# Second pass: where ScalarE clips the next unit's k

## The chip, the cores and the metric

The kernel runs on one core of a Trainium2 chip, in one launch, all in float32. The time is the device time of that core in microseconds, as the median of several runs.

## What is computed

Two layers run one after the other on x of shape (8, 256, 64, 64), batch by channels by rows by columns. The first is attention with keys and values from a strided 4x4 convolution. The second, the one that the change is in, is a linear attention with ReLU on q and k:

```
qkv = einsum('oc,bchw->bohw', w_qkv, x)
dw  = conv(qkv, w_dw, 5x5, per channel)
agg = einsum('goi,bgihw->bgohw', w_pw, dw)        # 96 groups of 8 channels
ms  = concatenate([qkv, agg], axis=1)
q, k, v = relu(ms[:d]), relu(ms[d:2d]), ms[2d:]   # per head, d = 8, v padded with a 1
kv  = einsum('bhnd,bhne->bhde', k, v)
out = einsum('bhnd,bhde->bhne', q, kv)
out = out[..., :-1] / (out[..., -1:] + 1e-15)
```

A projection, a normalization by fixed constants and the residual follow. Half of the heads read qkv itself ("raw" in the kernel), the other half read agg, what the 5x5 convolution and the 8x8 mix make of it. The ReLU on k is "the clipping" in what follows.

## The kernel before

Three passes share one program. The first (L575) does layer 0 and the qkv projection and stores qkv in DRAM in several layouts. The second (L961) makes the sums over tokens, kv, for all heads, and the whole output of the agg half. The third (L1279) applies the raw half, projects, and writes the output.

The second pass goes over 64 units: t in 2, k in 4, batch b in 8, one unit being 32 heads' channels of one batch. Its loop (L1225) is a software pipeline. In its step u it works on four units at once: u (convolution of k), p = u - 1 (token sums of agg), q = u - 2 (convolution of q) and r = u - 3 (application of the sums). What the steps of this text touch:

- load_tokens(u) (L1002) loads the raw k of a unit into kq (512 KB) and raw v into vq. kq has two buffers, used in turn.
- positive(u) (L1066) clips kq in place on ScalarE (L1068, 128x1024), then has GpSimd add it up over tokens: reduced (L1059), lines L1061 to L1063, into red_raw, which has one buffer.
- summed_raw(u) (L1104) is 32 small matmuls of kq with vq (L1110). ended_raw(u) (L1153) adds one matmul with red_raw (L1157) and copies the result out on VectorE (L1159, L1160).
- convolve(u, what, i) (L1073) is 16 matmuls into a PSUM bank: what = 1 is k (L1085), what = 0 is q (L1089). There are three banks of the tag cv, taken in turn. Part i = 2 comes first and ScalarE copies it to `both` (L1092). Parts 0 and 1 are added to `both` on VectorE (L1100, s) and clipped on ScalarE (L1101, r).
- summed(u) (L1120) is 32 matmuls of r with vq (L1127), four side by side in the four column strips of the array. A reduction on GpSimd (red_agg, again L1061 to L1063) and small work on VectorE (L1137 to L1145) follow. ended (L1167) and spread (L1175) turn the sums into the block matrix bd, by two small matmuls (L1170, L1177), a copy on ScalarE (rep, L1179) and two products on GpSimd.
- applied(u, par) (L1196) multiplies q by bd into ng (L1201). Then ScalarE's den (L1203), VectorE's reciprocal (L1204), product tok (L1206) and transpose att (L1213) follow each other.
- paired(u, what) (L1020) makes the differences c on VectorE (L1025, L1026), and on GpSimd a copy (L1029).

The source gives the calls in an order, but the framework's planner orders each engine's instructions when the program is built, by its own reckoning of when they can start. An engine then runs its instructions in that order. An instruction given to `tc.keep_in_program_order` stays at its place in the source among its engine's instructions; before, only some stores are given to it. In the order as built before, ScalarE's clipping that stands between r of convolve(q, 0, .) and `both` of convolve(u, 1, 2) is that of k two units ahead of the raw matmuls around it, though the source calls positive(u) at the head of step u.

Of the kernel before, what the change touches and what calls it, by code (L numbers as in the profile page):

```python
# [28 lines left out]
AF = mybir.ActivationFunctionType  # L29
# [931 lines left out]
def second_pass(ctx: ExitStack, tc: tile.TileContext, a, planes, kd, vd, wtd, kvd, attd):  # L961
    nc = tc.nc
# [16 lines left out]
    def bank(tag, name, bufs=1, n=512):  # L979
        return psums[tag].tile([P, n], F32, tag=tag, name=name, bufs=bufs)  # L980

    units = [(t, k, b) for t in range(2) for k in range(4) for b in range(B)]
    n_all = len(units)
# [10 lines left out]
    def load_cells(u, what):  # L994
        t, k, b = units[u]
        home = (second if u % 2 else first) if what else third
        d = home.tile([P, 4, (NB + 1) ** 2], F32, tag=f"d{what}_{u % 2}", name=f"d{what}_{u}")
        nc.sync.dma_start(d, planes[b, 2 * what + t][4 * k : 4 * k + 4].rearrange("g p e -> p g e"))
        grids[u, what] = d.rearrange("p g (y x) -> p g y x", x=NB + 1)


    def load_tokens(u):  # L1002
        t, k, b = units[u]
        kq = (second if u % 2 else first).tile([P, 2, 4, P], F32, tag=f"kq_{u % 2}", name=f"kq_{u}")
        nc.sync.dma_start(
            kq.rearrange("p a c e -> p a (c e)"),
            kd[b][4 * t + k].rearrange("a y (m i) b e -> (y m) a (i b e)", i=2),
        )
        kqs[u] = kq
        vq = (second if u % 3 else first).tile([P, 4, 6 * P], F32, tag=f"vq_{u % 3}", name=f"vq_{u}")  # L1010
        v = vd[b][4 * t + k]
        row = (NB2 + 2) * P
        for r in range(4):
            src = [[2 * row, NB], [4 * P, NB // 2], [1, 6 * P]]
            nc.sync.dma_start(vq[:, r], bass.AP(tensor=v.tensor, offset=v.offset + r * row, ap=src))
        vqs[u] = vq.rearrange("p r (c f h e) -> p r c f h e", c=6, f=4, h=4)
# [3 lines left out]
    def paired(u, what):  # L1020
        d = grids[u, what]
        c = (pairs if what else late).tile([P, 2 + what, 4, (NB + 1) * NB // 2], F32, tag=f"c{what}", name=f"c{what}_{u}")
        v = c.rearrange("p n g (y x) -> p n g y x", x=NB // 2)
        d0, d1, d2 = (d[:, :, :, i : i + NB - 1 : 2] for i in range(3))
        nc.vector.tensor_sub(v[:, 0], d0, d1)  # L1025
        nc.vector.tensor_sub(v[:, 1], d2, d1)  # L1026
        if what:

            nc.gpsimd.tensor_copy(v[:, 2], d1)  # L1029
        cells[u, what] = c  # L1030
# [28 lines left out]
    def reduced(u, what, t):  # L1059
        r = mid.tile([P, 4, P], F32, tag=f"red_{what}", name=f"red_{what}_{u}", bufs=1)  # L1060
        nc.gpsimd.tensor_tensor(r, t[0], t[1], ALU.add)  # L1061
        nc.gpsimd.tensor_tensor(r[:, :2], r[:, :2], r[:, 2:], ALU.add)
        nc.gpsimd.tensor_tensor(r[:, 0], r[:, 0], r[:, 1], ALU.add)  # L1063
        reds[u, what] = r[:, 0]

    def positive(u):  # L1066
        kq = kqs[u]
        nc.scalar.activation(kq, kq, AF.Relu)  # L1068
        reduced(u, "raw", (kq[:, 0], kq[:, 1]))


# [1 line left out]
    def convolve(u, what, i):  # L1073
        t, k, b = units[u]
        c, w, d = cells[u, what], wt[t, k, what], grids[u, what]
        ps = bank("cv", f"cv{what}_{u}_{i}", 3)
        for g in range(4):
            for da in range(2):
                n = 2 * da + i if i < 2 else 4 + da
                cols = slice(da * (NB // 2), da * (NB // 2) + P)  # L1080
                x = d[:, g, da : da + NB, 1:NB:2] if i == 2 and not what else c[:, i, g, cols]
                m = w[:, g, n * P : (n + 1) * P]
                out = ps[:, g * P : (g + 1) * P]
                if what:
                    nc.tensor.matmul(out, x, m, start=(da == 0), stop=(da == 1))  # L1085
                else:
                    if i == 2:
                        out = out.rearrange("p (y x) -> p y x", y=NB)
                    nc.tensor.matmul(out, m, x, start=(da == 0), stop=(da == 1))  # L1089
        if i == 2:  # L1090
            both = between.tile([P, QB], F32, tag="both", name=f"both{what}_{u}")
            nc.scalar.copy(both, ps)  # L1092

            r = (sides if what else two).tile([P, 2, 4, P], F32, tag=f"r{what}", name=f"r{what}_{u}")
            state[u, what] = (r, both)
            (kts if what else qs)[u] = r
        else:
            r, both = state[u, what]
            s = sides.tile([P, QB], F32, tag="s", name=f"s{what}_{u}_{i}")
            nc.vector.tensor_add(s, ps, both)  # L1100
            nc.scalar.activation(r[:, i].rearrange("p h n -> p (h n)"), s, AF.Relu)  # L1101


    def summed_raw(u):  # L1104
        kq, vq = kqs.pop(u), vqs[u]
        ps = bank("raw", f"raw_{u}")
        for i in range(8):
            r, c = i // 4, i % 4
            for f in range(4):
                nc.tensor.matmul(  # L1110
                    ps[f * D0 : (f + 1) * D0, :D0],
                    kq[:, r, c, f * D0 : (f + 1) * D0],
                    vq[:, r + 1, c + 1, f].rearrange("p h e -> p (h e)"),
                    start=(i == 0),
                    stop=(i == 7),
                )
        raws[u] = ps
# [45 lines left out]
    def stored_raw(u):  # L1163
        t, k, b = units[u]
        tc.keep_in_program_order(nc.sync.dma_start(kvd[b, t][:, k], mraws.pop(u)))
# [30 lines left out]
    def applied(u, par):  # L1196
        t, k, b = units[u]
        q, bd = qs[u], bds[u]
        pn = bank("ng", f"ng_{u}_{par}", 1, 1024).rearrange("p (h n) -> p h n", h=4)
        for h in range(4):  # L1200
            nc.tensor.matmul(pn[:, h, : P + 16], q[:, par, h], bd[:, h], start=True, stop=True)  # L1201
        den = late.tile([P, 2, 4, 16], F32, tag="den", name=f"den_{u}_{par}")
        nc.scalar.activation(den[:, 0], pn[:, :, P : P + 16], AF.Identity, bias=eps)  # L1203
        nc.vector.reciprocal(den[:, 1], den[:, 0])  # L1204
        tok = late.tile([P, 16, D0], F32, tag="tok", name=f"tok_{u}_{par}")
        nc.vector.tensor_tensor(  # L1206
            tok.rearrange("p f (h e) -> p h f e", e=D1),
            pn[:, :, :P].rearrange("p h (f e) -> p h f e", e=D1),
            den[:, 1].unsqueeze(3).to_broadcast([P, 4, 16, D1]),
            ALU.mult,  # L1210
        )
        att = two.tile([P, 512], F32, tag="att", name=f"att_{u}_{par}", bufs=4)
        nc.vector.transpose(att, tok.rearrange("p f e -> p (f e)"))  # L1213
        done[u, par] = att


    def stored(u, par):
        t, k, b = units[u]
        c0 = P * t + D0 * k
        tc.keep_in_program_order(  # L1220
            nc.sync.dma_start(attd[b][c0 : c0 + D0, par].rearrange("c j n -> j c n"), done.pop((u, par)))
        )

    paired(0, 1)
    for u in range(n_all + 3):  # L1225
        p, q, r = u - 1, u - 2, u - 3
        now, was, conv, out = u < n_all, 0 <= p < n_all, 0 <= q < n_all, 0 <= r < n_all
        if now:
            positive(u)
            if u > 0:  # L1230
                summed_raw(u)
        if u + 1 < n_all:
            load_tokens(u + 1)
        if 0 < p < n_all:
            load_cells(p, 0)
        if was:
            stored_raw(p)
        if r > 0:
            stored(r - 1, 0)
            stored(r - 1, 1)  # L1240
        if was:
            summed(p)
        if now:
            convolve(u, 1, 2)
        if out:
            applied(r, 0)
        if u + 1 < n_all:
            paired(u + 1, 1)
        if now:
            convolve(u, 1, 0)  # L1250
            if u == 0:
                summed_raw(u)
            ended_raw(u)
            convolve(u, 1, 1)
        if u + 2 < n_all:
            load_cells(u + 2, 1)
        if was:
            ended(p)
        if conv:
            paired(q, 0)  # L1260
            convolve(q, 0, 2)
        if out:
            applied(r, 1)
        if conv:
            convolve(q, 0, 0)
        if was:
            spread(p)
        if conv:
            convolve(q, 0, 1)
        if now and u + B < n_all:  # L1270
            b = units[u][2]
            load_weights(u + B - b, 1 if b < 4 else 0, b % 4)
# [354 lines left out]
```

## Time and profile before

| what | us |
|---|---|
| median of 3 runs | 4081.7 (4080.74 to 4086.17) |
| span of the profiled run | 4083.3 |
| TensorE matmul busy | 3951.4 |
| VectorE busy | 1901.1 |
| ScalarE busy | 1651.8 |
| GpSimd busy | 1193.4 |
| the second pass, first raw matmul to last row of ng | 2139.2 to 3427 |
| one clipping, L1068 (64 of them) | 1.06 |

In the profile, PE is TensorE's matmuls and PEld its weight loads, DVE is VectorE, ACT ScalarE, POOL GpSimd, SPq the queue that issues the DMAs. A row of the trace in order of time has start, duration, engine, line of the kernel, operation, output<-input, shape and count; merged rows carry the count x. A bracket at its end gives how long that engine was idle before it and what ended the wait. A wait in a list is told as the waiting row, the arrow, and the row that released it. Float32 matmuls stand in the trace as two records each.

### The profile page before, as it was taken

The page shows a single profiled execution, that of the slowest core. Times are in us where ns is not written, and L with a number is a line of the kernel's source. Part 1 is how long each engine was busy: PE and PEld are TensorE (multiplying, and loading weights), DVE is VectorE, ACT ScalarE, POOL GpSimd, SP SyncE. Part 2 cuts the span into 40 slices and gives each one's busy share as a digit, 9 for nine tenths or more (in the row PEclk, how much of TensorE's full clock was granted, in tenths as well). Part 3 has the DMA queues.
Part 4 walks back from the last instruction along what each step waited for, and adds up shares of the span by engine and source line. Part 5 has one row for each costly group of instructions (what it writes and reads, how often), then busy time and mean ns, then how long its engine had stood idle before and what let it go on. Part 6 is the DMA issues. An engine that isn't in the chain of part 4 may idle for free. (4 is left out here: it accounts for less than half of the span.)

```text
span 4083.3 us, 69412 instructions
## 1 busy us (share of the span) xinstructions
PE 3951.4 (97%) x27266; PEld 2340.8 (57%) x27266; DVE 1901.1 (47%) x2724; ACT 1651.8 (40%) x3505; POOL 1193.4 (29%) x1234
## 2 busy tenths in 40 slices
PE   8999999999999999999998899999999998999998
PEld 4433434434334343343347788888888886555655
DVE  2554344343443434344445555555555554444443
ACT  2345454453554545545542222222222223445544
POOL 2323233233333323323334343333433431000000
PEclk9999999999999999999999999999999999999999
DMA  7655435344353443534449877777777766777674
GB/s 234 205 178 163 117 91 151 94 121 133 94 147 100 114 137 100 139 97 116 136 117 267 233 207 215 215 204 227 214 206 226 200 178 166 225 210 229 196 235 136
DMA packets 588320, 691.31 MB, mean 169 GB/s; under 512 B 62160, under 2 KB 431312, under 8 KB 583760
## 3 DMA queue, kind: packets, MB, share of 16 engines
q1 hardware_dynamic: 587984, 686.79, 59.2%
q8 instruction: 216, 3.54, 0.4%
q14 instruction: 120, 0.98, 0.1%
HBM read 412.54 MB, written 274.10 MB: 168 GB/s over the span
## 5 line engine op out<-in xcount | busy, mean ns | idle before, releaser
L786 POOL TENSOR_TENSOR e<-e,e 128x512 f32<-128x512 f32 x512 | 651.1, 1304 | 1204.5 <-PE av L775 1190.9
L799 DVE RECIPROCAL rden<-den 128x512 f32<-128x512 f32 x128 | 429.7, 3357 | 688.0 <-PE den L791 688.0
L834 PE MATMUL qkv<-x,wqkv 128*128 128x512 f32 x1536 | 700.4, 599 | 0.0
L764 ACT ACTIVATE e<-sc 128x512 f32<-128x512 f32 x1024 | 529.1, 603 | 421.0 <-PE sc L758 421.0
L834 PEld LDWEIGHTS qkv<-x,wqkv 128*128 128x128 f32 x1536 | 285.1, 190 | 372.4 <-issue 353.7
L1085 PE MATMUL cv<-w,c 128*128 128x128 f32 x3072 | 387.8, 280 | 7.9 <-POOL c L1029 5.3
L1085 PEld LDWEIGHTS cv<-w,c 128*128 128x128 f32 x3072 | 361.6, 193 | 36.6 <-issue 30.7
L853 DVE STREAM_TRANSPOSE turned<-qkv 128x512 f32<-128x512 f32 x256 | 177.4, 707 | 338.5 <-ACT stage L843 285.4
L758 PE MATMUL sc<-q,kk 32*128 32x512 f32 x2048 | 323.6, 640 | 10.7 <-DVE x L810 7.8
L1101 ACT ACTIVATE r<-s 128x512 f32<-128x512 f32 x256 | 159.7, 631 | 332.7 <-DVE s L1100 325.5
L1450 DVE TENSOR_TENSOR y<-z,xs 128x256 f32<-128x256 f32 x256 | 144.4, 652 | 312.0 <-ACT z L1441 292.3
L1068 ACT ACTIVATE kq<-kq 128x1024 f32<-128x1024 f32 x64 | 67.6, 1057 | 538.7 <-DMA kq<-k 406.0
L775 PE MATMUL av<-e,vv 128*32 128x512 f32 x2048 | 274.8, 609 | 0.0
L843 ACT COPY stage<-qkv 128x512 f32<-128x512 f32 x256 | 149.9, 585 | 301.8 <-PE qkv L834 296.4
L1127 PE MATMUL sums<-vq,r 128*32 128x288 f32 x4096 | 263.5, 409 | 2.4 <-ACT r L1101 2.4
L1441 ACT ACTIVATE z<-p,bn 128x256 f32<-128x256 f32 x256 | 133.7, 578 | 312.3 <-PE p L1432 238.2
L743 PE MATMUL q<-x,wq 128*128 128x512 f32 x512 | 254.3, 619 | 1.0 <-ACT stage L843 1.0
L1089 PE MATMUL cv<-c,w 128*128 128x128 f32 x2048 | 253.8, 278 | 0.0
L1432 PE MATMUL p<-att,wproj 128*128 128x512 f32 x512 | 249.4, 609 | 1.9 <-ACT att L1415 1.9
L1204 DVE RECIPROCAL den<-den 128x64 f32<-128x64 f32 x128 | 70.8, 553 | 369.2 <-ACT den L1203 369.1
L671 PE MATMUL sr<-x,wsr 128*128 128x256 f32 x1024 | 234.7, 385 | 6.8 <-DMA wsr<-in_w_sr_dram 6.8
L1432 PE MATMUL p<-agg,wproj 128*128 128x512 f32 x512 | 241.3, 594 | 0.0
(121 smaller groups left out, 5260.2 us busy)
## 6 DMA issues: line engine op xcount, KB each, us to landing
vq<-v SPq DMA_DIRECT2D x256, 384.0 KB
planes<-stage SPq DMA_DIRECT2D x256, 289.0 KB
d<-planes SPq DMA_DIRECT2D x128, 578.0 KB
raw<-planes SPq DMA_DIRECT2D x128, 272.0 KB
x<-in_xp_dram SPq DMA_DIRECT2D x64, 512.0 KB
wsr<-in_w_sr_dram SPq DMA_DIRECT2D x128, 256.0 KB
x<-x SPq DMA_DIRECT2D x128, 256.0 KB
k<-turned SPq DMA_DIRECT2D x256, 128.0 KB
```

Of the source, the lines that this page charges most:

```text
L671: nc.tensor.matmul(ps[:, oc], w[:, ci, oc * P : (oc + 1) * P], xt[:, ci, f * NK : (f + 1) * NK], start=(f == ci == oc == 0), stop=(f == R ...
L743: nc.tensor.matmul(ps, consts["wq"][:, ci, c * P : (c + 1) * P], x_tiles[b][:, ci, s * QB : (s + 1) * QB], start=(ci == 0), stop=(ci == 1),)
L758: nc.tensor.matmul(scs[h], kks[b][rows, c, kc * P : (kc + 1) * P], qs[rows], start=True, stop=True)
L764: nc.scalar.activation(e, scs[h], AF.Exp, scale=D0**-0.5)
L775: nc.tensor.matmul(sums["av"][cols], vvs[b][:, kc, c * P + h * D0 : c * P + (h + 1) * D0], es[h], start=(kc == 0), stop=(kc == 1),)
L786: nc.gpsimd.tensor_tensor(es0[h], es0[h], es1[h], ALU.add)
L799: nc.vector.reciprocal(r, den)
L834: nc.tensor.matmul(ps, consts["wqkv"][:, ci, j * P : (j + 1) * P], x_tiles[b][:, ci, s * QB : (s + 1) * QB], start=(ci == 0), stop=(ci == 1),)
L1085: nc.tensor.matmul(out, x, m, start=(da == 0), stop=(da == 1))
L1089: nc.tensor.matmul(out, m, x, start=(da == 0), stop=(da == 1))
L1127: nc.tensor.matmul(ps[h * D0 : (h + 1) * D0, : 36 * D1].rearrange("p (r n e) -> p r n e", r=3, e=D1), kt[:, par, h, 2 * r + c], vq[:, r : ...
L1432: nc.tensor.matmul(ps.rearrange("p (f q n) -> p f q n", f=4, q=4), wproj[:, j, oc * P : (oc + 1) * P], src, start=(j == 0), stop=(j == 3),)
```

## The change

The clipping is moved and pinned. In step u, positive(u + 1) is now called late in the step, after convolve(q, 0, 0) and ahead of spread(p), and its ScalarE instruction is given to keep_in_program_order, so the planner can't draw it forward. positive(0) is called ahead of the loop. The aim is that ScalarE doesn't come to a clipping whose k is still being loaded, and doesn't hold up what is queued behind it. Nothing else is edited; the instructions are the same in number and shape.

```
     def positive(u):
         kq = kqs[u]
-        nc.scalar.activation(kq, kq, AF.Relu)
+        tc.keep_in_program_order(nc.scalar.activation(kq, kq, AF.Relu))
         reduced(u, "raw", (kq[:, 0], kq[:, 1]))
...
+    positive(0)
     paired(0, 1)
     for u in range(n_all + 3):
         p, q, r = u - 1, u - 2, u - 3
         now, was, conv, out = u < n_all, 0 <= p < n_all, 0 <= q < n_all, 0 <= r < n_all
-        if now:
-            positive(u)
-            if u > 0:
-                summed_raw(u)
+        if 0 < u < n_all:
+            summed_raw(u)
         if u + 1 < n_all:
             load_tokens(u + 1)
...
             applied(r, 1)
         if conv:
             convolve(q, 0, 0)
+
+        if u + 1 < n_all:
+            positive(u + 1)
         if was:
             spread(p)
         if conv:
```

In the order as built after the change, ScalarE's clipping stands between the two rows of r (L1101) of convolve(q, 0, 0) and convolve(q, 0, 1) and is that of the next unit's k. GpSimd's three red_raw rows follow bd's two. TensorE has five of the 32 matmuls of summed(p) ahead of the 32 raw matmuls of that next unit and 27 behind them, where all 32 stood behind before.

More of the change, by code (lines that the diff above doesn't have):

```diff
@@ L1067, in positive @@
         kq = kqs[u]
-        nc.scalar.activation(kq, kq, AF.Relu)
+        tc.keep_in_program_order(nc.scalar.activation(kq, kq, AF.Relu))
         reduced(u, "raw", (kq[:, 0], kq[:, 1]))
@@ L1222, in stored @@
         )
+    positive(0)
     paired(0, 1)
@@ L1227, in second_pass @@
         now, was, conv, out = u < n_all, 0 <= p < n_all, 0 <= q < n_all, 0 <= r < n_all
[L1228 to L1231, printed above, removed]
+        if 0 < u < n_all:
+            summed_raw(u)
         if u + 1 < n_all:
@@ L1265, in second_pass @@
             convolve(q, 0, 0)
+        if u + 1 < n_all:
+            positive(u + 1)
         if was:
```

## The prediction

> **What bounds the kernel now.** I read the page's engine shares first, then busy time by stage, then the waits of the engine that bounds, then one unit of the second pass in order of time.
>
> ```profile
> PE 3951.4 (97%) x27266; PEld 2340.8 (57%) x27266; DVE 1901.1 (47%) x2724; ACT 1651.8 (40%) x3505; POOL 1193.4 (29%) x1234
> ```
>
> PE (TensorE) is the bound, so the change is worth what it does to PE's idle time. The columns by stage are the stretch, its length, and busy time of PE, PEld, DVE, ACT, POOL:
>
> ```profile
> 2139.00:2312.00 173.00, 151.11 (x1972) 131.89 (x1971) 88.98 (x168) 40.80 (x75) 67.37 (x77) 0.94 0.92 251
> 2312.00:3360.00 1048.00, 988.60 (x13054) 890.03 (x13055) 590.32 (x1168) 271.69 (x530) 412.71 (x479) 0.99 0.75 211
> ```
>
> The second stretch is 53 like units of the second pass (first raw matmul 2312.23 to 3359.88: 19.77 us a unit). PE idles 59.4 us there. Its waits, then ScalarE's longest one, in that stretch (us in total, times, longest):
>
> ```profile
> PE cv L1089 <- ACT both L1092: 59.2, 48, 3.0
> ```
> ```profile
> ACT kq L1068 <- DMA kq<-k: 351.9, 39, 10.6
> ```
>
> All of PE's idle time is one wait: the first matmul of convolve(q, 0, 2) for ScalarE's copy `both`. ScalarE's own long wait is the clipping of k (L1068), for its DMA. One unit shows the link:
>
> ```profile
> 2429.84 4.09 PE L1127 MATMUL sums<-vq,r 128*32 128x288 f32 x64
> ...
> 2430.06 0.67 SPq L1005 DMA_DIRECT2D kq<-k  x1
> ...
> 2433.86 2.05 PE L1085 MATMUL cv<-w,c 128*128 128x128 f32 x16
> ...
> 2440.52 0.28 PE L1170 MATMUL few<-ones,red_agg 128*128 128x1 f32 x2
> 2440.61 1.06 ACT L1068 ACTIVATE kq<-kq 128x1024 f32<-128x1024 f32 x1 [9.40 <-DMA kq<-k]
> ...
> 2441.58 0.57 ACT L1092 COPY both<-cv 128x512 f32<-128x512 f32 x1
> ...
> 2442.20 2.24 PE L1089 MATMUL cv<-d,w 128*128 128x128 f32 x16 [1.39 <-ACT both L1092]
> ```
>
> The k issued at 2430.06 lands ten us later, and ScalarE stands at its clipping until then. `both`, whose matmuls ended about 2435.9, is queued behind it and gives up its PSUM bank at 2442.15. convolve(q, 0, 2) needs that bank (the tag cv has three, and three convolve groups lie between), so PE stands 1.39 us. In the built order of before, the clipping in unit u is that of k(u+2), which raw (L1110) reads only at 2470.86: it is far too early.
>
> **What the Trainium skill says.** "TensorE: Matmul & The Clock Gate", on the array's architecture, calls ScalarE's and VectorE's queues strictly first in, first out. The trace agrees: `both` starts 0.97 us after the clipping does, though ready five us before. The same page's part on the HAM clock gate says that an idle window of about 3.4 us brings the slow clock. Here shorter stalls do it at times: after the 1.76 us stall at 2462.47 the granted clock was 0.74 in the next 4 us and convolve(q, 0, 2) took 3.62 us where 2.23 is usual; after 2.24 us at 2504.44 it stayed at 1.00. "ScalarE: Activation LUTs", on the cost of an ACTIVATE, gives 186 ns + 0.833 ns an element and 93 ns of overlap: 1039 ns for 1024 elements; the trace has 1057 and about 0.1 of overlap. "TensorEngine Tiling (Array Packing)", on the 128x32 mode, has four independent tiles. The trace agrees: 64 sums matmuls of 0.41 us each start within 4.02 us.
>
> **The change, part by part.** No instruction is added or removed, on any engine: 64 clippings of 1.06 us stay. The built orders differ in steady state in three places.
>
> (1) ScalarE: the clipping leaves its place ahead of `both` of convolve(u, 1, 2). That takes away PE's 59.2 us. Five units also had the slower clock behind their stall: 53 units less the stalls and at the stall-free period of 18.51 us leave 1047.65 - 59.2 - 981.0 = 7.4 us. Gain in steady state: 66.6 us. The 18.51 is built from T, the start of convolve(q, 0, 2): raw at T+6.93; raw's issue 0.61; sums 4.02; then 6.95 to the next T (2433.86 to 2442.20 less 1.39).
>
> (2) The clipping, now of k(u+1), stands between the two halves of r (L1101) of convolve(q, 0, .), and raw(u+1) on PE follows within the microsecond. That is a new wait. No clipping delays the second last unit, so its times, from T = 3371.32, are those of the new chain:
>
> ```profile
> 3371.32 2.22 PE L1089 MATMUL cv<-d,w 128*128 128x128 f32 x16
> ...
> 3374.62 0.31 ACT L1203 ACTIVATE den<-ng,eps 128x64 f32<-128x64 f32 x1 [0.40 <-PE ng L1201]
> ...
> 3374.97 0.55 DVE L1204 RECIPROCAL den<-den 128x64 f32<-128x64 f32 x1 [2.76 <-ACT den L1203]
> ...
> 3376.99 0.65 DVE L1100 TENSOR_TENSOR s<-cv,both 128x512 f32<-128x512 f32 x1
> ...
> 3377.68 0.63 ACT L1101 ACTIVATE r<-s 128x512 f32<-128x512 f32 x1 [0.94 <-DVE s L1100]
> ...
> 3378.25 0.73 PE L1110 MATMUL raw<-vq,kq 128*32 128x32 f32 x62
> ```
>
> den starts at T+3.30, VectorE's reciprocal, product, transpose and sum follow, r's first half starts at T+6.36. The clipping starts 0.54 later (0.63 less the overlap), T+6.90, ends T+7.96, and PE resumes 0.05 later (as behind `both`), T+8.01.
>
> (3) PE: the order puts five of the 32 sums matmuls (two records each) ahead of raw: 5/32 of 4.02 is 0.63, so PE reaches raw at T+7.56 and waits about **0.45 us a unit**. The cut also breaks a round of four tiles. Of the 27 sums left, 27/32 of 4.02 is 3.39; as seven rounds of 0.50 it is 3.52. Unit after: 8.01 + 0.61 + 3.39 to 3.52 + 6.95 = 18.96 to 19.09, so 0.45 to 0.58 above 18.51. I take 0.55, near the upper end since all three column tiles must start their round anew: 53 x 0.55 = 29 us given back. Steady net: 66.6 - 29.2 = 37 us.
>
> Early units (2222 to 2312): stalls behind late clippings of 0.22 + 0.72 + 2.27 + 2.38 + 4.70 + 0.53 = 10.8 us, one slow clock of 1.4; five new waits give back 2.8. Of the 9.4 I take 6, since DMA is 92% busy there and another load may come last. The last raw adds 0.5. Sum: 37 + 6 - 0.5 = 43 us; 4081.7 - 43 = **4039 us**.
>
> Costed at nothing: r's second half, 1 us later, is read by applied two convolve groups on (T+14). red_raw on GpSimd (1.27 + 0.73 + 0.45) now follows the clipping and ends about T+10.5; its reader L1157 on PE comes about 8 us after raw. The next k is issued when red_raw has read its buffer, some 2.7 us later than now, but has over 15 us before its clipping. The loads queued behind it (vq) wait for sums anyway. The move of clipping 0 from the first pass to its end falls into 1.5 us of ScalarE idle ahead of 2137.58.
>
> **The rivals.** *No new wait* (clipping done before PE gets there): for it, only 0.45 us separates them, and a shorter VectorE chain would close it; against, every term is measured without disturbance. Time: 4081.7 - 66.6 - 9 = 4006, with the cut round alone (0.13 a unit) 4013. *The wait moves rather than shrinks*: the chain den to clipping has six links on two engines, and 0.35 to 0.7 us of lag makes it 0.9 to 1.25 a unit: 4058 to 4078. *Slower*: the two c differences (2 x 0.72) that stand ahead of the reciprocal on VectorE start late, as their d lands late, and shift the chain by 1.44: 58 units x 1.99 = 115, less 76 gained: 4121. Against it, c waits for d only 0.9 us in 53 units.
>
> **How the numbers follow.** Forecast 0.68 (4025 to 4055), no wait 0.12, moved wait 0.12 (nearly all still faster), slower 0.08. The range 4012 to 4066 takes in the no-wait case with the cut round, the 0.45 and 0.58 ends, and half of the moved wait.
>
> **What would show it.** ScalarE's wait L1068 for DMA gone, PE's L1089 for `both` gone, a new PE (or PEld) wait of raw L1110 for ACT kq L1068 of 0.4 to 0.6 us about 58 times, no slow clock in the steady stretch, period near 19.05. Wrong, if PE waits for anything else more than 5 us, or raw's wait is above 0.9.

## The result, and the profile after

The changed kernel takes 4035.8 us (median of 4 runs, 4033.51 to 4040.05) against 4081.8 for the kernel before (4 runs): a ratio of 0.9887, 95% interval 0.9869 to 0.9904. The gain is 46.0 us; 43 was predicted.

The first view is again the engine shares, with the same instructions as before:

```profile
PE 3967.1 (98%) x27266; PEld 2322.3 (58%) x27266; DVE 1943.0 (48%) x2724; ACT 1666.0 (41%) x3505; POOL 1207.0 (30%) x1234
```

Then busy time by stage (stretch, length, PE, PEld, DVE, ACT, POOL, granted clock, DMA share, GB/s): the early units, and the steady ones up to the second last raw.

```profile
2139.00:2312.00 173.00, 159.39 (x2054) 135.27 (x2054) 89.59 (x168) 42.00 (x76) 70.30 (x80) 0.94 0.92 252
2312.00:3320.00 1008.00, 1007.82 (x13104) 879.60 (x13103) 641.08 (x1181) 285.84 (x535) 426.20 (x479) 1.00 0.76 219
```

In the steady stretch PE's idle time went from 59.4 us to 0.2. Read alone, that says that nothing is left to win there. The waits of the same stretch correct it; this is all that PEld and PE show of waits (us in total, times, longest):

```profile
PEld cv L1085 <- issue: 24.6, 53, 0.5
PEld raw L1110 <- ACT kq L1068: 23.3, 53, 0.7
```
```profile
PE raw L1110 <- ACT kq L1068: 0.2, 1, 0.2
```

Both rows that carried the prediction are gone: PE no longer waits for `both`, and ScalarE no longer waits for k's DMA there. The first row above is no news: the kernel before has it too (23.7 us from 2312 to 3320). The new wait of raw for the clipping is there in every unit, 0.44 us each (23.3 / 53), almost wholly on the weight loads. PE counts as busy meanwhile, because the records of sums matmuls already loaded run on (the ends of matmul records are modelled in this profile, not seen); the first half microsecond of such a wait stands on PEld alone, as the second experiment shows. One unit in order of time, from T = 2447.87:

```profile
2447.87 2.22 PE L1089 MATMUL cv<-d,w 128*128 128x128 f32 x16
...
2451.17 0.31 ACT L1203 ACTIVATE den<-ng,eps 128x64 f32<-128x64 f32 x1 [0.40 <-PE ng L1201]
...
2454.22 0.63 ACT L1101 ACTIVATE r<-s 128x512 f32<-128x512 f32 x1 [0.94 <-DVE s L1100]
...
2454.76 1.04 ACT L1068 ACTIVATE kq<-kq 128x1024 f32<-128x1024 f32 x1
...
2454.80 1.16 PE L1127 MATMUL sums<-vq,r 128*32 128x288 f32 x10
...
2455.85 0.64 PEld L1110 LDWEIGHTS raw<-vq,kq 128*32 128x32 f32 x63 [0.43 <-ACT kq L1068]
```

The clipping has no bracket any more: ScalarE comes to it from r and does not idle. The ten sums records (five matmuls) start, then the weight load of raw waits 0.43 us for the clipping, which ends at 2455.80.

The steady unit, from the 10th raw to the 63rd (2304.79 to 3305.50, 53 units), is 18.88 us against 19.77, and nearly every one is between 18.86 and 18.89. In the profiled runs, whose spans differ by 51.6 us (4083.3 and 4031.7), the gain falls out so: 1.9 us up to the first raw, 5.5 in the nine early units, 46.9 in the 53 steady ones; 0.5 is lost in the last unit and 2.3 after the last raw.

### The profile page after: what moved, and what is told of

Its sections match the earlier page's. It is cut to its first block, busy times and chain, and to the rows that moved or that the text cites. A ratio compares the mean times of both kernels' runs of the same rounds, so it can differ in the third digit from the quotient of the medians.

```text
span 4031.7 us, 69469 instructions
## 1 busy us (share of the span) xinstructions
PE 3967.1 (98%) x27266; PEld 2322.3 (58%) x27266; DVE 1943.0 (48%) x2724; ACT 1666.0 (41%) x3505; POOL 1207.0 (30%) x1234
## 5 line engine op out<-in xcount | busy, mean ns | idle before, releaser
L1127 PE MATMUL sums<-vq,r 128*32 128x288 f32 x4096 | 303.1, 410 | 0.0
L1101 ACT ACTIVATE r<-s 128x512 f32<-128x512 f32 x256 | 160.5, 627 | 299.9 <-DVE s L1100 299.5
L1092 ACT COPY both<-cv 128x512 f32<-128x512 f32 x128 | 75.0, 586 | 421.8 <-PE cv L1085 364.8
L1089 PEld LDWEIGHTS cv<-c,w 128*128 128x128 f32 x2048 | 242.2, 194 | 0.0
```

The costliest lines, as they stand in the source:

```text
L1127: nc.tensor.matmul(ps[h * D0 : (h + 1) * D0, : 36 * D1].rearrange("p (r n e) -> p r n e", r=3, e=D1), kt[:, par, h, 2 * r + c], vq[:, r : ...
```

## The experiments

The theory: ScalarE runs its instructions in order, so what counts is where the clipping stands. Too early, it waits for k's DMA and holds `both`, and so PSUM's bank and PE; too late, it makes raw wait. Rivals: the place in the source or the number of buffers, k's transfer itself, ScalarE's amount of work, or TensorE's own work at the break. The table has the time, its ratio to the runs of the kernel before on the same chip (95% interval), and the steady unit, read as above in each trace; the kernel before had medians of 4079.3 and 4079.7 us there.

| kernel | us | ratio | steady unit |
|---|---|---|---|
| moved, not pinned | 4082.6 | 1.0009 (1.0001 to 1.0017) | 19.67 |
| pinned, not moved | 4037.7 | 0.9897 (0.9879 to 0.9915) | 18.84 |
| before, three buffers for k | 4085.7 | 1.0013 (1.0007 to 1.0020) | 19.68 |
| before, both on VectorE | 4057.5 | 0.9952 (0.9938 to 0.9965) | 19.22 |
| clipping behind den(1) | 4006.4 | 0.9818 (0.9805 to 0.9832) | 18.32 |
| clipping ahead of r1 | 4004.6 | 0.9819 (0.9804 to 0.9834) | 18.36 |
| behind den(1), clipped twice | 4005.7 | 0.9814 (0.9800 to 0.9827) | 18.37 |
| changed, clipping in halves | 4033.0 | 0.9894 (0.9879 to 0.9909) | 18.92 |

**Moved, not pinned.** The change without its pin:

```
-        tc.keep_in_program_order(nc.scalar.activation(kq, kq, AF.Relu))
+        nc.scalar.activation(kq, kq, AF.Relu)
```

> The changed kernel without the pin: the source keeps the clipping late in the unit, but the planner may place it where it likes. By the planned order ScalarE clips k(u+2) ahead of both in the steady units again, as in the kernel before. Theory (the pin decides, the place in the source does nothing by itself): the waits for k's DMA and TensorE's stalls at the third convolution are back, unit 19.77 us, 4078 to 4083. Rival (the move in the source, with the earlier summed part, is what brought the gain): 4036.

Measured 4082.6 us. ScalarE's wait and PE's, from 2312 to 3280:

```profile
ACT kq L1068 <- DMA kq<-k: 368.5, 41, 11.0
...
PE cv L1089 <- ACT both L1092: 51.4, 41, 3.1
```

Both old waits are back. The planner draws the clipping ahead again, and the move in the source alone brings nothing.

**Pinned, not moved.** The kernel before with the pin alone, the clipping at the head of the unit that uses it:

```
-        nc.scalar.activation(kq, kq, AF.Relu)
+        tc.keep_in_program_order(nc.scalar.activation(kq, kq, AF.Relu))
```

> The kernel before with the pin alone, the clipping left at the head of the unit that uses it. By the planned order ScalarE clips k(u) behind both halves of r0 and ahead of the next both, about 1.4 us later than in the changed kernel, and TensorE has 16 of the 32 sums ahead of raw to fill the time, where the changed kernel has 5. Theory (the clipping out of the way of both is the whole gain; a late clipping makes raw wait, the sums ahead of it fill that): a wait of 0.4 to 0.6 us per unit at raw, unit 18.8 to 19.0, 4032 to 4042. Rival (the clipping's later place lengthens the wait by the 1.4 us that it comes later): unit near 20.2, 4100 or above.

Measured 4037.7 us, the changed kernel's time within the intervals. The pin is the gain; of the two places tried with it, neither is better. Its trace shows why a clipping behind both halves of r costs no more than one between them:

```profile
2460.36 2.61 PE L1127 MATMUL sums<-vq,r 128*32 128x288 f32 x34
...
2461.73 1.04 ACT L1068 ACTIVATE kq<-kq 128x1024 f32<-128x1024 f32 x1
2462.82 0.64 PEld L1110 LDWEIGHTS raw<-vq,kq 128*32 128x32 f32 x63 [0.39 <-ACT kq L1068]
```

Here 17 sums (34 records; not the 16 of the expectation) stand ahead of raw, not five. They fill the time by which the clipping comes later, and the wait left is 0.39 us.

One early unit of the same trace has a long wait at this place, and shows how much of it PE's records hide:

```profile
2253.54 0.64 PEld L1110 LDWEIGHTS raw<-vq,kq 128*32 128x32 f32 x63 [2.39 <-ACT kq L1068]
2253.54 0.75 PE L1110 MATMUL raw<-vq,kq 128*32 128x32 f32 x63 [1.85 <-ACT kq L1068]
```

Of the 2.39 us that PEld waits, PE shows 1.85; the other 0.54 are the records of the sums ahead. At this place a wait under 0.54 us doesn't appear on PE at all.

**Before, with three buffers for k.**

```
-        kq = (second if u % 2 else first).tile([P, 2, 4, P], F32, tag=f"kq_{u % 2}", name=f"kq_{u}")
+        kq = (second if u % 3 else first).tile([P, 2, 4, P], F32, tag=f"kq_{u % 3}", name=f"kq_{u}")
```

> The kernel before with three buffers for k's tokens instead of two, so that k's transfer may start a unit sooner. By the planned order the clipping is then drawn forward by a further unit, to k(u+3), and stands ahead of both just as before. Theory (the planner puts a clipping that it may move as early as the buffers allow, so a buffer more moves the wait and doesn't take it away): waits for k's DMA on ScalarE and TensorE's stalls stay, unit near 19.8, 4075 to 4090. Rival (the transfer is merely one unit late, and a buffer more hides it): unit 18.3 to 18.6, 4010 to 4025.

Measured 4085.7 us: no gain. ScalarE's clipping ahead of `both` is that of k(u+3) and waits as before (341.3 us for the DMA from 2312 to 3280, 38 times), and PE waits 51.7 us for `both`. With two buffers as with three, the unpinned clipping moves up as far as the buffers let it.

**Before, with both on VectorE.** Only the copy of the third convolution is taken out of ScalarE's queue:

```
-            nc.scalar.copy(both, ps)
+            if what:
+                nc.vector.tensor_copy(both, ps)
+            else:
+                nc.scalar.copy(both, ps)
```

> The kernel before with one edit: VectorE instead of ScalarE copies both of the third convolution (what = 1) out of its bank. The early clipping of k(u+2) stays in ScalarE's queue and still waits there for k's DMA; only both no longer stands behind it. Theory (TensorE stalls because both, which frees the bank, is queued behind the waiting clipping; the DMA wait itself is harmless): ScalarE's waits for k's DMA stay at 300 us or more, TensorE's waits for both are gone, the steady unit falls from 19.77 us to between 18.3 and 18.7, 4005 to 4030 in all. Rival (the transfer of k, or the load on the DMA engines in that stretch, holds the unit whatever stands in the queue): unit 19.77, 4075 to 4085. Second rival (what else stands behind the waiting clipping, den and r0, takes both's place): unit 19 to 19.5, 4040 to 4065.

Measured 4057.5 us: the second rival's number, not the theory's 4005 to 4030. First ScalarE's wait for the DMA, then what PE waits for, from 2312 to 3280 (line numbers behind L1092 are three higher in this kernel's file):

```profile
ACT kq L1068 <- DMA kq<-k: 349.7, 39, 11.5
...
PE ng L1204 <- DVE tok L1209: 22.3, 23, 2.6
```

PE's wait for `both` is gone although ScalarE waits for k as long as before; so the transfer as such does not hold PE. But the next in the queue takes its place:

```profile
2532.73 1.06 ACT L1068 ACTIVATE kq<-kq 128x1024 f32<-128x1024 f32 x1 [8.81 <-DMA kq<-k]
...
2533.70 0.30 ACT L1206 ACTIVATE den<-ng,eps 128x64 f32<-128x64 f32 x1
2534.03 0.55 DVE L1207 RECIPROCAL den<-den 128x64 f32<-128x64 f32 x1 [4.73 <-ACT den L1206]
2534.68 0.69 DVE L1209 TENSOR_TENSOR tok<-ng,den 128x512 f32<-128x512 f32 x1
```

den starts as the clipping ends, VectorE's reciprocal had waited 4.73 us for it, and tok follows, which PE's next ng waits for. So it is the whole of ScalarE's queue that the early clipping holds up. The 22.3 us are about half of what this kernel's units lie above 18.31 us (0.91 each, some 46 in the stretch); where the rest goes was not followed up. The order of the rows agrees with what the Trainium skill says in "TensorE: Matmul & The Clock Gate", on the array's architecture: ScalarE's queue is strictly first in, first out.

**The clipping behind den(1).** In the changed kernel, two lines exchanged:

```
         if out:
             applied(r, 1)
+        if u + 1 < n_all:
+            positive(u + 1)
         if conv:
             convolve(q, 0, 0)
-
-        if u + 1 < n_all:
-            positive(u + 1)
```

> The changed kernel with the pinned clipping of k(u+1) moved one place forward, ahead of the third convolution's last part, so that ScalarE runs it right behind den(1) and ahead of the two halves of r0, about 1.5 us earlier in the unit than in the changed kernel; all 32 sums then stand behind raw. Theory that the clipping's place in ScalarE's queue decides: the wait of raw for it (0.50 us per unit against a stall-free unit of 18.37 us) goes, the steady unit falls from 18.88 to 18.37, and 53 units at 0.50 give about 27 us: 4006 to 4010. Rival (what is left in the unit is TensorE's own work, the wait at raw only the record of a weight load that runs ahead): the unit stays near 18.88 and the time near 4036. Second rival (the clipping ahead of r0 delays r0 and with it the sums): the wait moves to the sums, 0.5 to 1 us per unit, 4036 to 4060.

Measured 4006.4 us, faster than both kernels. Its busy times from 2312 to 3280, in the columns above, and one unit:

```profile
2312.00:3280.00 968.00, 967.92 (x13013) 874.89 (x13012) 595.10 (x1167) 288.91 (x530) 419.53 (x477) 1.00 0.80 228
```
```profile
2459.39 2.21 PE L1089 MATMUL cv<-d,w 128*128 128x128 f32 x16
...
2462.68 0.31 ACT L1203 ACTIVATE den<-ng,eps 128x64 f32<-128x64 f32 x1 [0.40 <-PE ng L1201]
...
2462.89 1.05 ACT L1068 ACTIVATE kq<-kq 128x1024 f32<-128x1024 f32 x1
...
2465.73 0.63 ACT L1101 ACTIVATE r<-s 128x512 f32<-128x512 f32 x1 [0.94 <-DVE s L1100]
...
2466.30 0.64 PEld L1110 LDWEIGHTS raw<-vq,kq 128*32 128x32 f32 x63
```

The clipping lies in time in which ScalarE waited for VectorE, ends 2.36 us ahead of raw, and raw starts at T+6.91 with no bracket. PE is as busy as in the changed kernel, yet the unit is 0.56 us shorter, at 18.32 (most units 18.30 or 18.31): the changed kernel's 1007.8 busy of 1008 us held half a microsecond of waiting in each unit.

**The clipping ahead of r1.** Earlier still, behind applied(r, 0):

```
         if out:
             applied(r, 0)
         if u + 1 < n_all:
+            positive(u + 1)
+        if u + 1 < n_all:
             paired(u + 1, 1)
...
-        if u + 1 < n_all:
-            positive(u + 1)
```

> The changed kernel with the pinned clipping of k(u+1) put still earlier, behind the first applied part of unit r and ahead of the two halves of r1. Theory that any place after k has landed and before raw wants it is as good as another: unit 18.37 us, total within 5 us of the kernel that clips right behind den(1), 4006 to 4010. Rival: the landing of k is not yet sure there, ScalarE waits for its DMA again, both and the third convolution are held as in the kernel before, and the time goes back toward 4082. Second rival: r1 comes 1 us later and the sums of unit r wait for it, 4036 or above.

Measured 4004.6 us with a unit of 18.36: no wait of ScalarE for k's DMA in the steady stretch, and none of the sums. Of the places tried behind the landing of k, the two that leave room ahead of raw are equally good; the changed kernel's and that of the pin alone come too late.

**Behind den(1), clipped twice.**

```
         tc.keep_in_program_order(nc.scalar.activation(kq, kq, AF.Relu))
+        tc.keep_in_program_order(nc.scalar.activation(kq, kq, AF.Relu))
```

> The kernel that clips right behind den(1), with every clipping done twice: 64 times 1.05 us, 67 us more of ScalarE's work at the place where nothing waits for it. Theory (the place in the queue decides, the amount of work on ScalarE does not, with 1 us to spare there): unit 18.3 to 18.5, 4005 to 4015. Rival (ScalarE's amount of work counts, off TensorE's path too): 60 us more, 4065 or above. Between them, if the second clipping delays r0 so far that raw or the sums wait for it: 0.5 to 0.6 us per unit, 4035 to 4040.

Measured 4005.7 us, with ScalarE busy for 60.8 us more (1731.6 against 1670.8; the two clippings overlap a little). So this much more work costs nothing there. The 46 us of the change, which adds and takes away no work, came from the place.

**The changed kernel with the clipping in halves.**

```
-        tc.keep_in_program_order(nc.scalar.activation(kq, kq, AF.Relu))
+        for i in range(2):
+            tc.keep_in_program_order(nc.scalar.activation(kq[:, i], kq[:, i], AF.Relu))
```

> The changed kernel with its clipping cut in two pinned halves of 128x512 at the same place. The first half of raw needs only the first of them, which ends some 0.4 us sooner (about 0.6 us for a half, as 1.04 us for the whole). Theory (the unit above 18.31 us, which the two kernels with earlier clipping reach, is raw's wait for the clipping's end): the 0.57 us that the changed kernel has above it falls by about 0.4, 53 units give 21 us, 4012 to 4020. Rival (the 0.57 is mostly the price of raw standing between sums, after the fifth of 32): 4030 to 4037, and no lower.

Measured 4033.0 us and a unit of 18.92: not the theory's 4012 to 4020 but the rival's 4030 to 4037, of a price for raw's standing between the sums. The trace offers another reason:

```profile
2455.04 1.14 ACT L1069 ACTIVATE kq<-kq 128x512 f32<-128x512 f32 x2
...
2455.08 0.69 PE L1128 MATMUL sums<-vq,r 128*32 128x288 f32 x8
...
2455.71 0.35 PEld L1111 LDWEIGHTS raw<-vq,kq 128*32 128x32 f32 x32 [0.47 <-ACT kq L1069]
...
2455.95 0.14 PEld L1128 LDWEIGHTS sums<-vq,r 128*32 128x32 f32 x2
...
2456.23 0.54 PEld L1111 LDWEIGHTS raw<-vq,kq 128*32 128x32 f32 x32
...
2460.26 1.86 PEld L1086 LDWEIGHTS cv<-w,c 128*128 128x128 f32 x16 [0.47 <-issue]
```

Raw's first half does start 0.42 us sooner (0.63 behind the first sums, where raw starts 1.05 behind them in the changed kernel). But the last half of the clipping ends at 2456.18, 1.14 behind its start where one whole takes 1.04, and raw's second half starts at 2456.23. From there to the next convolution it takes 4.03 us, with half of raw to do; in the changed kernel, 4.09 with all of it (2455.85 to 2459.94). Raw is so short (0.56 us from its first load to the next sums) that half of it, with another change between raw and sums, saves next to nothing. So the end of the whole clipping can have been the limit, and not its first half; this run alone doesn't decide between that and the rival.

What speaks against the rival is in the traces of the changed kernel and of the pin alone. In every unit there in which raw's is the only wait, the stretch from the first sums to the next convolution is raw's bracket and 4.71 us, to 0.01: 5.10 with a bracket of 0.39, 5.14 with 0.43, 5.42 with 0.71, 7.10 with 2.39. The wait is paid in full. In the kernel that clips behind den(1), where raw stands ahead of all sums and doesn't wait, the stretch is 4.58, which leaves 0.13 for the break. No unit has raw between sums without a wait, though (the smallest bracket is 0.38), so what the break would cost then was not measured.

## Why the prediction was right, point by point

**What bounds** held: PE, through ScalarE's queue. Moved without the pin the wait returns, with `both` out of the queue PE's wait for it goes while the DMA wait stays, and twice the work in a good place costs nothing.

**(1) What the old place cost** was put at 66.6 us and is 77: 19.77 - 18.31 = 1.46 us a unit, times 53. The stall-free unit of 18.51 was the mis-sized term. It took 6.95 us from the next convolution to the next T, by subtracting the listed stall of 1.39 from a unit that had one; in the changed kernel this stretch is 6.81 (2441.06 to 2447.87). The reason is in how a bracket is counted:

```profile
2447.73 0.28 PE L1170 MATMUL few<-ones,red_agg 128*128 128x1 f32 x2
2447.87 2.22 PE L1089 MATMUL cv<-d,w 128*128 128x128 f32 x16
```

Without a stall the convolution starts 0.14 us before the record ahead of it ends. A bracket begins at that end, so the time lost is the bracket and 0.14, whatever its length: in the kernel before, 6.95 is left behind a stall of 0.11 us (2794.08 to 2801.14) as behind one of 2.98 (2812.65 to 2822.57). The unit that the prediction took for (2), with T at 3371.32, had no stall, and has the 6.81 too (from 3364.51). Most of the rest is 0.05: raw and sums together take 4.58 (2448.00 to 2452.58 in the kernel that clips behind den(1)), not 0.61 + 4.02.

**(2) The new chain** held to 0.03 us: den T+3.30, r T+6.35, clipping T+6.89, raw T+7.98, where T+3.30, T+6.36, T+6.90 and T+8.01 stood.

**(3) What is given back** was put at 0.55 us a unit and is 0.57 (18.88 against 18.31), 30 us in 53 units where 29 stood. The stretch from the first sums to the next convolution shows it whole: 5.14 us (2454.80 to 2459.94) against 4.58. Of the 0.56, 0.43 is the bracket at raw, for 0.45, and 0.13 is left for the break, as much as the prediction gave the broken round alone. The pin alone, with 17 sums ahead, also cuts a round of four behind its first matmul, and has the same 0.13; a cut between two rounds was not tried, so that the broken round is its cause is not shown.

So the steady net was 47 us, not 37; the unit of 18.88 lies under the 18.96 to 19.09 of the prediction by that 0.14, and by 0.03 in the chain. **The early units** gave 5.5 for 6. Of the stalls left there, one of 4.9 us is raw's wait for the clipping (from the list of PE's waits from 2139 to 2312):

```profile
PE raw L1110 <- ACT kq L1068: 5.1, 2, 4.9
```

Ahead of it, c on VectorE waits 4.28 us for d's DMA: the mechanism of the slower rival, and the only time that it cost PE microseconds. Not for want of late d: from 2312 to 3320 c waits for d 15 times, 42.2 us in all, where the prediction counted on the 0.9 us of before, and yet raw's wait never goes above 0.7 us there. Not forecast were 1.9 us gained up to the first raw and 2.3 lost after the last one, which no experiment looked into. The profiled pair is 51.6 apart and the medians 46.0, since the profiled execution of before was 3.3 us above its median and that of after 2.3 below. Beside a scatter of that size, the nearness of 43 to 46 owes something to luck: the ten microseconds by which the forecast for the steady stretch was too small are a real miss.

**Two readings** in the prediction are off, without a share in its sum. The granted clock of 0.74 is that of 2464 to 2468; in the 4 us from 2462.47 it was 0.57. And between convolve(u, 1, 2) and convolve(q, 0, 2) stand two convolve groups, not three, so that the fourth group comes back to the first one's bank.

**The rivals.** No new wait, 4006 us, was not this kernel's case, but it is where the clipping behind den(1) lands. The moved wait and the slower case did not come. The slow clock is gone in the steady stretch, as forecast: 1.00 on average.

## What to carry to other kernels

An instruction that waits for a DMA on an in-order engine costs whatever is queued behind it: look at what follows it, and pin it where its input has surely landed, the engine would idle anyway, and its reader is still some way off. Taking out one of the instructions behind it let the next one wait here (22 us gained, where a good place gained 73), and adding a buffer while the planner could still draw it forward brought nothing. When a change removes a stall, take the stall-free time from a unit that had none, and look for short new waits on the weight loads, where a busy PE hides them.

## What the runs showed of the hardware beyond that

- A bracket on TensorE leaves out the overlap of records: each stall ahead of these 128x128 matmuls cost 0.14 us more than its bracket, from 0.11 us of stall to 2.98.
- PE was 99.98% busy in a stretch that could still be shortened by 3% (18.88 to 18.31 us a unit), as the records of the 128x32 matmuls ahead cover the first 0.54 us of a wait.
- Cutting one 128x1024 activation in two 128x512 cost 0.10 us in all (1.14 for 1.04 us), so the halving as such was cheap.
